# The second product of a ConvNeXt V2 block in 15 block products instead of 18, with the response normalisation applied to its input

## The chip, the cores and the metric

The kernel runs on one core of one Trainium2 chip. The metric is device time in microseconds (us) for one execution. All engines of the core work on their own instruction streams and wait for each other by semaphores: TensorE (matmuls), VectorE, ScalarE, GpSimd and SyncE, which here only issues transfers. In the profile they are PE (with PEld for the loads of stationary weights), DVE, ACT, POOL and SP; L12 is line 12 of the kernel.

## The reference, cut to what matters

Eight images of 384 channels and 32 x 32 positions pass through two layers in fp32. Layer 0 is a transformer block; layer 1 is a ConvNeXt V2 block. The change is mostly in the last lines of layer 1.

```python
# layer 0, per image, xf = positions x channels
x1 = attention(layernorm(xf)) + xf             # 8 heads of 48
h  = gelu(layernorm(x1) @ w_fc1.T + b_fc1)     # 384 -> 1536
x  = x1 + h @ w_fc2.T + b_fc2                  # 1536 -> 384
# layer 1, per image
y = depthwise_conv_7x7(x) + dw_b
y = layernorm(y)
y = gelu(y @ w1 + b1)                          # 384 -> 1536
gx = sqrt(sum(square(y), over the positions))  # one per channel
nx = gx / (mean(gx over channels) + 1e-6)
y = grn_gamma * (y * nx) + grn_beta + y        # response normalisation
out = x + y @ w2 + b2                          # 1536 -> 384
```

The response normalisation multiplies each of the 1536 channels by one factor, 1 + gamma * nx, known only when the whole image's gelu is done. grn_beta is folded into b2 once, in image 0.

## The kernel before, in words

Channels lie on the 128 partitions, positions along the free dimension: 384 channels are 3 tiles, 1536 are 12, an image has N = 1024 positions in two halves of NH = 512. A matmul is 128x128 weights by 128x512 activations. The loop `main` (L1442) takes the images in order; image b runs layer 0: `qk` (L442), `attention` (L537), `mlp` (L760) with fc1 and then `fc2` (L783), `keep` (L913, which stores x in DRAM). Then layer 1 of image b-1 runs: `grn_up` (L950, w1 and gelu), `values` (L472, the v projection of the next image) and `grn_down` (L1143, w2). The depthwise convolution of image b is 147 taps of 128x1024 on VectorE (L936), spread under the TensorE work of the next image. Images 6 and 7 go through w2 by `grn_down_straight` (L1023), 72 matmuls an image.

The order of the instructions is written out when the program is built. `Flow` (L111) keeps a clock that advances by U = 0.857 us for each 128x512 matmul emitted; chains of small steps (Python generators) yield how long they want to wait, and are continued when the clock has come that far. A paced chain counts its waits from when it was due, `flow.finish` emits all that is left of a chain at once. So what an engine does next is fixed by the planner's clock, not by who is ready.

Two fast block schemes save matmuls. `fc2` cuts h into three parts of four tiles by two halves of positions (b11 to b32) and computes 15 products of four matmuls each, p0 to p14, with sums of weight blocks (`FORMS`, L73) made once in image 0 by `prepare` (L1225) and kept in DRAM as s_fc2. The products' other operands are sums of activation blocks: e, f, g, h and d in the code, with e', f', f'', h' and g' here for the later values that overwrite them. VectorE makes those with pairs of 128x1024 sums (`both_pairs`, L816), or a GpSimd transfer adds one block to another in place (`adding`, L823). `grn_down` calls `down` (L671) instead: the third rows straight (24 matmuls) and seven products of six. Its operands t1 and t3 are differences by ScalarE (times -1) and a GpSimd accumulating transfer (`difference`, L661); t2 and t4 are VectorE's. The factors of the response normalisation are applied to w2: `scaled` (L1117) multiplies six weight tiles by them on VectorE as they come, and `grn_sums` (L1127) adds four sums of the scaled weights. `grn_scale` (L1095) makes the factors.

`down` adds x as residual from six loads of 256 KB (`load` in `grn_down`), adding the bias as it goes (L1153), and stores each block when it is complete. SyncE issues weight loads into a ring of nine tiles (`Weights`, L249), x and residual loads and stores in program order. PSUM results of products alternate between a pool of two double banks and a pool of four.

## Time and profile before

| what | value |
|---|---|
| median of 3 runs | 3422.79 us (3420.5 to 3424.79) |
| the profiled execution, its own time | 3430.41 us |
| its span | 3428.6 us |
| TensorE busy | 3362.1 us, 98% |
| VectorE busy | 2496.0 us, 73% |
| ScalarE busy | 1372.7 us, 40% |
| GpSimd busy | 142.2 us, 4% |
| transfers | 259.53 MB, mean 76 GB/s |

A group of instructions is given by line, engine and operation, then what it writes and reads, its count, its busy time and the mean length of one; the idle time before it and what released it follow. In the timeline a line is start, length, engine, line, operation, with the idle time just before it and its releaser in brackets. A matmul of 128x512 in fp32 shows as two records of TensorE (some records can be missing). The chain of waits follows the last instruction back to what released it; pieces in order of time are start, length, what. The busy table gives a stretch's bounds, its length, and the busy time and count of PE, PEld, DVE, ACT and POOL, then the granted TensorE clock, the share of the transfer engines and GB/s.

### The profile page before, as it was taken

The numbers are of one execution on the slowest core, as the hardware profiler recorded it, in microseconds if no ns is written. First come the engines' busy times: TensorE is split into PE (matmuls) and PEld (weight loads), VectorE is DVE, ScalarE is ACT, GpSimd is POOL, SyncE is SP. The second block draws the span as 40 slices with busy tenths as digits, with TensorE's granted clock in tenths as the row PEclk, the third lists the DMA queues.
The fourth block names the chain that finished last, engine by engine and source line by source line (L and its number), as shares of the span: only waits on it lengthen the run. The fifth ranks groups of instructions, "written<-read, shape, count | busy, mean of one in ns | idle before, by whom it ended". The sixth has DMA issues, their size and how long they took to land.

```text
span 3428.6 us, 36855 instructions
## 1 busy us (share of the span) xinstructions
PE 3362.1 (98%) x14194; PEld 1441.4 (42%) x14194; DVE 2496.0 (73%) x3040; ACT 1372.7 (40%) x1814; POOL 142.2 (4%) x155
## 2 busy tenths in 40 slices
PE   8999999999999999999999999999999999999999
PEld 3334434443344433444334443344434444344455
DVE  3343888777878778778787786977879679959950
ACT  2442353333534245341543515525154342531631
POOL 0201000000000000000001000010000000000000
PEclk9999999999999999999999999999999999999999
DMA  3415201641026410353005430054300642013231
GB/s 103 150 56 123 65 17 36 164 105 39 21 60 156 101 26 21 83 155 89 17 16 118 129 82 19 13 132 121 82 13 23 156 105 68 14 53 87 65 91 54
DMA packets 138952, 259.53 MB, mean 76 GB/s; under 512 B 33424, under 2 KB 35856, under 8 KB 138384
## 3 DMA queue, kind: packets, MB, share of 16 engines
q1 hardware_dynamic: 109424, 191.69, 18.8%
q0 software_dynamic: 28768, 62.92, 9.8%
q8 instruction: 114, 1.87, 0.2%
q10 hardware_dynamic: 576, 2.48, 0.2%
q14 instruction: 70, 0.57, 0.1%
HBM read 168.68 MB, written 30.41 MB: 58 GB/s over the span
## 4 chain that ended last, share of the span: by engine, by line
PE 81%; DVE 10%; DMA 2%; issue 1%; SPq 1%; ACT 1%; POOL 0%; DVEq 0%; POOLq 0%; ACTq 0%
PE fc L345 11%; PE s L548 10%; PE o L568 10%; PE h L352 10%; PE fc_p L352 9%; PE qk L332 5%; PE o L1043 4%; PE o_S L352 4%; PE o_straight L704 4%; PE v L477 3%; PE proj L491 3%; DVE acc L936 3%; DVE wqkv L936 3%; PE o_A L352 3%; PE h_last L1087 2%; PE ln_var L401 1%
## 5 line engine op out<-in xcount | busy, mean ns | idle before, releaser
L936 DVE SCALAR_TENSOR_TENSOR acc<-pad,vec,acc 128x1024 f32<-128x1024 f32 x1008 | 1230.9, 1275 | 0.0
L557 ACT ACTIVATE p<-s 128x1024 f32<-128x1024 f32 x512 | 523.2, 1023 | 390.4 <-PE s L548 390.0
L548 PE MATMUL s<-qk 48*64 48x512 f32 x4096 | 537.5, 593 | 1.7 <-ACT qk L451 1.5
L568 PE MATMUL o<-p,v 64*64 64x512 f32 x4096 | 531.7, 591 | 0.0
L345 PE MATMUL fc<-xn,fc 128*128 128x512 f32 x1152 | 503.3, 595 | 1.3 <-DVE x L758 1.2
L345 PEld LDWEIGHTS fc<-xn,fc 128*128 128x128 f32 x1152 | 218.5, 190 | 280.3 <-issue 272.8
L352 PE MATMUL fc_p<-hid,fc 128*128 128x512 f32 x728 | 323.4, 595 | 9.5 <-issue 9.5
L985 DVE TENSOR_TENSOR y<-h,y 128x512 f32<-128x512 f32 x288 | 198.4, 691 | 112.6 <-PE h L352 101.7
L548 PEld LDWEIGHTS s<-qk 48*64 48x64 f32 x4096 | 152.4, 133 | 295.9 <-issue 272.2
L568 PEld LDWEIGHTS o<-p,v 64*64 64x64 f32 x4096 | 157.1, 133 | 284.5 <-issue 279.6
L364 ACT ACTIVATE hid<-fc,bfc_f 128x512 f32<-128x512 f32 x192 | 130.8, 686 | 361.1 <-PE fc L345 360.9
L352 PEld LDWEIGHTS fc_p<-hid,fc 128*128 128x128 f32 x728 | 138.0, 190 | 186.4 <-issue 185.7
L332 PE MATMUL qk<-xn,wqkv 128*128 128x512 f32 x480 | 207.4, 592 | 0.0
L352 PE MATMUL h<-acc,w_A 128*128 128x512 f32 x432 | 204.0, 592 | 0.0
L936 DVE SCALAR_TENSOR_TENSOR wqkv<-pad,vec,wqkv 128x416 f32<-128x416 f32 (+1 forms) x288 | 193.4, 744 | 0.6
L451 ACT ACTIVATE qk<-qk,bqk 128x1024 f32<-128x1024 f32 x40 | 44.5, 1114 | 352.6 <-PE qk L332 352.6
L509 DVE TENSOR_TENSOR attn<-o,attn 128x512 f32<-128x512 f32 x64 | 44.1, 688 | 152.4 <-ACT attn L507 152.4
L491 PE MATMUL proj<-attn,wproj_sb 128*128 128x512 f32 x288 | 129.7, 603 | 11.2 <-DVE attn L535 11.2
L332 PEld LDWEIGHTS qk<-xn,wqkv 128*128 128x128 f32 x480 | 91.1, 190 | 114.1 <-issue 113.8
L477 PE MATMUL v<-wqkv,xn 128*128 128x384 f32 x384 | 129.0, 495 | 0.6 <-DVE xn L413 0.6
L352 PEld LDWEIGHTS h<-acc,w_A 128*128 128x128 f32 x432 | 82.1, 190 | 103.3 <-issue 99.0
L704 PE MATMUL o_straight<-y,w_A 128*128 128x512 f32 x288 | 124.6, 592 | 0.0
(254 smaller groups left out, 3299.2 us busy)
## 6 DMA issues: line engine op xcount, KB each, us to landing
w_A<-in_w SPq DMA_DIRECT2D x108, 384.0 KB, 3.2
fc<-s_fc SPq DMA_DIRECT2D x91, 256.0 KB, 2.8
hid<-hid POOLq DMA_DIRECT2D x42, 512.0 KB, 5.9
fc<-in_wfc SPq DMA_DIRECT2D x54, 384.0 KB, 3.4
xn<-in_x SPq DMA_DIRECT2D x16, 768.0 KB, 9.1
x<-in_x SPq DMA_DIRECT2D x16, 768.0 KB, 14.4
kept<-x SPq DMA_DIRECT2D x8, 1536.0 KB, 5.9
res<-kept SPq DMA_DIRECT2D x42, 256.0 KB, 3.5
```

The costliest lines, as they stand in the source:

```text
L332: nc.tensor.matmul(out=ps[:, half(h)], lhsT=lhsT(k), rhs=rhs(k)[:, half(h)], start=(k == 0), stop=(k == nk - 1),)
L345: nc.tensor.matmul(out=ps, lhsT=lhsT(k), rhs=rhs(k)[:, half(h)], start=(k == 0), stop=(k == nk - 1))
L352: nc.tensor.matmul(out=bank, lhsT=lhsT, rhs=rhs, start=k == 0, stop=k == len(pairs) - 1)
L477: nc.tensor.matmul(out=ps[:, :C], lhsT=xn[:, k, t * P : (t + 1) * P], rhs=wv_sb[:, k, :], start=(k == 0), stop=(k == CT - 1),)
L491: nc.tensor.matmul(out=ps, lhsT=wproj_sb[:, m, ct * P : (ct + 1) * P], rhs=attn[:, m, :], start=(m == 0), stop=(m == CT - 1),)
L548: nc.tensor.matmul(out=s[64 * i : 64 * i + 64, j, :], lhsT=kT[64 * j : 64 * j + HD, m, k0 : k0 + 64], rhs=qT[64 * j : 64 * j + HD, m, half ...
L557: nc.scalar.activation(p, s, AF.Exp)
L568: nc.tensor.matmul(out=outs[i][64 * j : 64 * j + 64, :], lhsT=v[keys, t, at : at + 64], rhs=p[keys, j, :], start=(t == 0), stop=(t == KT - 1),
L704: nc.tensor.matmul(out=straight[:, n, :], lhsT=a(key)[k], rhs=block(s, n)[k], start=s + k == 0, stop=s == 1 and k == h - 1,)
L936: nc.vector.scalar_tensor_tensor(dst, window, tap, dst, ALU.mult, ALU.add)
L985: nc.vector.tensor_tensor(dst, bank, part, ALU.add)
L1043: nc.tensor.matmul(out=ps, lhsT=tiles[k], rhs=y(k, part), start=(k == 0), stop=(k == HT - 1))
```

## The change

The change has five parts.

1. w2 of images 0 to 5 goes through fc2's scheme. `fc2` becomes `by_thirds`, called for both; `down`, `grn_sums`, `first_difference` and `spare_blocks` are gone. For w2 it makes e itself (`made` is False).
2. `prepare` makes the block sums of w2 too, after all else, by the same code, into s_w2. The waits in it grow from 10 to 16 and from 12 to 18.
3. The factors multiply y instead of w2: `grn_scale` emits twelve ScalarE multiplications of 128x1024 by a per-partition factor, between the copies of the v projection that runs then and on into the w2 stage.
4. The residual is one load of 1.5 MB into a tile with x's tag, before `grn_up`; products are added into it, and its six blocks are stored. The load of the next image's x stands behind `grn_down` now.
5. In `by_thirds`, so in fc2 too, h and e' are emitted earlier (h after f, during p2; e' right behind h) and f' directly after p6's first addition, not after p7.

The pace of the convolution is 1.6 instead of 1.55 in image 0, 1.46 instead of 1.42 in image 6.

```diff
@@ plan_w2
-        if not fast:
-            return [((f"w2_{tag}", a), chunk(w2, c)) for c, a in enumerate(RAW)]
-        return [
-            ((f"w2_{tag}", a), chunk(w2, RAW.index(a)) if a in RAW else None)
-            for a in ("A31", "A32", "A11", "A12", "A21", "S4", "S2", "S3", "A22")
-        ]
+        if fast:
+            return plan_thirds(f"w2_{tag}", w2, s_w2)
+        return [((f"w2_{tag}", a), chunk(w2, c)) for c, a in enumerate(RAW)]
@@ fc2
-    def fc2(b, xt, hid, e, weights, wname):
+    def by_thirds(xt, hid, e, made, weights, wname, column, done, name):
...
+        making_e = None if made else flow.spawn(both_pairs(e, b11, b12, ALU.subtract), paced=True)
         n16 = copy(spare[:, 0, :], product(b12))
         bias(2, c31, product(b21))
-        f = b21
+        flow.finish(making_e)
+        f, h = b21, b11
         making_f = flow.spawn(both_pairs(f, e, b21, ALU.subtract), paced=True)
+        making_h = flow.spawn(after(making_f, both_pairs(h, e, b31, ALU.subtract)), paced=True)
         p = product(e)
+        making_e = flow.spawn(after(making_h, both_pairs(e, h, b12)), paced=True)
         op(c31, p, c31)
         op(c21, c21, p, ALU.subtract)
         bias(2, c32, product(b22))
         flow.finish(making_f)
         g = b22
         adding(g, f)
-        h = b11
-        making_h = flow.spawn(both_pairs(h, e, b31, ALU.subtract), paced=True)
-        making_e = flow.spawn(after(making_h, both_pairs(e, h, b12)), paced=True)
         n17 = copy(spare[:, 1, :], product(f))
         flow.finish(making_h)
         n15 = copy(temporary("n15"), product(h))
         flow.finish(making_e)
         adding(h, b32)
         p = product(e)
         op(n15, p, n15)
+        flow.finish(flow.spawn(both_pairs(f, f, b12)))
         bias(0, c11, p)
...
         bias(1, c22, product(g))
         adding(g, b32)
-        making_f = flow.spawn(both_pairs(f, f, b12), paced=True)
         op(c11, product(b31), c11)
-        flow.finish(making_f)
         op(n17, product(f), n17, ALU.subtract)
         making_f = flow.spawn(after(None, both_pairs(f, f, g, ALU.subtract), 2.0), paced=True)
...
@@ grn_scale
-        for key in first:
-            scaled(b, weights.at(wb, key), key, key in spare)
+        if y is None:
+            for key in RAW[:2]:
+                scaled(b, weights.at(f"w2_{tag}", key), key, key == RAW[1])
+            return
+        yield 1.5
+        for m in range(HT):
+            nc.scalar.mul(y[:, m, :], y[:, m, :], scale[:, m : m + 1])
+            yield 1.1
@@ grn_down
+    def load_kept(b, kept):
+        t = one.tile([P, CT, N], F32, tag="x", name=f"kept_{b}")
+        nc.sync.dma_start(out=t, in_=kept.rearrange("(c p) n -> p c n", p=P))
+        return t
+
+    def grn_down(b, y, xt, weights, tag, index):
+        e = [three.tile([P, 2, NH], F32, tag="p", name=f"w2_e_{b}_{i}") for i in range(2)]
 
         def done(r, n):
-            if (r, n) == (2, 1):
-                flow.finish(sums)
-            nc.sync.dma_start(out=image_of(out, index)[r * P : (r + 1) * P, half(n)], in_=res.pop((r, n)))
-            if queue:
-                load(*queue.pop(0))
...
-        down(y, y1, weights, f"w2_{tag}", first, add, done, f"o2_{b}")
+            nc.sync.dma_start(out=image_of(out, index)[r * P : (r + 1) * P, half(n)], in_=xt[:, r, half(n)])
+
+        by_thirds(xt, y, e, False, weights, f"w2_{tag}", lambda r: b2[:, r : r + 1], done, f"o2_{b}")
@@ prepare
+        def forms(name, w, store):
...
+        yield from forms("fc2", wfc2, s_fc2)
         weights.release()
...
+        yield from forms("w2", w2, s_w2)
@@ main
+            if b == 0:
                 xt = load_x(b + 1, "x")
-            if b == 0:
                 flow.finish(preparing)
-                start_conv(b, 1.55)
+                start_conv(b, 1.6)
                 next_values(1)
                 continue
+            if b < B - 1:
+                xt = load_kept(b - 1, kept.pop(b - 1))
             flow.finish(state["norm3"])
             if b < B - 1:
-                y, y1, gx = grn_up(b - 1, acc, weights, b - 1)
-                start_conv(b, 1.42 if b == B - 2 else 1.8, 10)
-                scale = flow.spawn(grn_scale(b - 1, gx, weights, b - 1))
+                y, gx = grn_up(b - 1, acc, weights, b - 1)
+                start_conv(b, 1.46 if b == B - 2 else 1.8, 10)
+                scale = flow.spawn(grn_scale(b - 1, gx, weights, b - 1, y))
                 next_values(b + 1)
                 flow.finish(scale)
-                grn_down(b - 1, y, y1, kept.pop(b - 1), weights, b - 1, b - 1)
+                grn_down(b - 1, y, xt, weights, b - 1, b - 1)
+                xt = load_x(b + 1, "x")
```

## The prediction

> **What bounds the kernel.** The page's busy row and its chain first:

> ```profile
> PE 3362.1 (98%) x14194; PEld 1441.4 (42%) x14194; DVE 2496.0 (73%) x3040; ACT 1372.7 (40%) x1814; POOL 142.2 (4%) x155
> ...
> PE 81%; DVE 10%; DMA 2%; issue 1%; SPq 1%; ACT 1%; POOL 0%; DVEq 0%; POOLq 0%; ACTq 0%
> ```

> TensorE is busy 98%, and 9 tenths or more in every slice but the first: a matmul less is time less, a late operand is time more. Next the chain of waits through the second image's w2 (start, length, line, records):

> ```profile
> 1132.91 7.74 PE v L477 x24
> 1140.65 0.12 PE gxsum L1102 x2
> 1140.77 7.84 PE v L477 x24
> 1148.61 20.60 PE o_straight L704 x48
> 1169.21 10.30 PE o_A L352 x24
> 1179.51 20.60 PE o_S L352 x48
> 1200.11 5.15 PE o_A L352 x12
> ```

> Four pieces join without a gap into 56.65 us: 132 records, 66 matmuls of 128x512, two records each, so 0.858 us a matmul. The stage's rows in the busy table (us of PE, PEld, DVE, ACT, POOL), of the second and the sixth image:

> ```profile
> 1148.61:1205.26 56.65, 56.65 (x134) 25.08 (x133) 47.95 (x53) 4.24 (x5) 3.57 (x3) 1.00 0.43 109
> 2804.89:2861.54 56.65, 56.65 (x133) 25.08 (x133) 54.78 (x59) 4.24 (x5) 3.57 (x3) 1.00 0.43 109
> ```

> VectorE is nearly full here already, with the next convolution's taps, which can wait. Last, where TensorE does wait: fc2, in the timeline of one image:

> ```profile
> 1036.89 2.07 DVE L413 SCALAR_TENSOR_TENSOR acc<-acc,vec,ln_rstd 128x512 f32<-128x512 f32 x3
> ...
> 1038.88 2.07 DVE L413 SCALAR_TENSOR_TENSOR acc<-acc,vec,attn 128x512 f32<-128x512 f32 x3
> ...
> 1040.86 1.22 DVE L816 TENSOR_TENSOR fc_e<-hid 128x1024 f32<-128x1024 f32 x1
> ...
> 1042.14 1.98 PE L352 MATMUL fc_p<-fc_e,fc 128*128 128x512 f32 x4 [0.77 <-DVE fc_e L816]
> ...
> 1050.67 2.35 DVE L816 TENSOR_TENSOR hid<-hid 128x1024 f32<-128x1024 f32 x2
> ...
> 1051.99 4.53 PE L352 MATMUL fc_p<-hid,fc 128*128 128x512 f32 x10 [1.00 <-issue]
> ```

> The second half of e' sits behind six normalisation operations and costs 0.77; f' is made just before its product and costs 1.00 ("issue", but the product starts as f' is ready). Image 0 has 3.11 before the same product (at 332.19). The page's groups agree: 9.5 of idle before the L352 matmuls that read hid (6 x 1.00 + 3.1 and little else), 4.6 = 6 x 0.77 before those that read fc_e.

> [...] the trace has 1216 and 690. In a row they start 1.13–1.14 and 0.61 apart, read from the timeline.

> **Removed.** 18 products become 15 of four matmuls: 60 instead of 66, six images: 6 x 6 x 0.858 = −30.9. Scaling and summing weights on VectorE, the t1 and t3 differences and six residual loads go too; none holds TensorE in the rows above, so they only make room.

> **fc2.** In the shared code e' is queued straight after h, during the third product, ahead of the normalisations; f' follows p6's first operation rather than standing before p9. If both stalls go: 6 x (0.77 + 1.00) + 3.1 = −13.7.

> **Factors on ScalarE.** Let 0 be the start of the stage's first product (1148.61 above).

> ```profile
> 1141.74 0.17 DVE L1110 TENSOR_SCALAR gscale<-gscale 128x12 f32<-128x12 f32 x1
> ...
> 1142.85 0.48 ACT L485 COPY v<-v 128x384 f32<-128x384 f32 x1 [1.68 <-PE v L477]
> ...
> 1144.78 0.48 ACT L485 COPY v<-v 128x384 f32<-128x384 f32 x1 [1.46 <-PE v L477]
> ```

> The scale is ready at −6.7; ScalarE has 1.45 between v copies. No row has a 1024-wide multiply by a pointer; [...] the nearest rows have 1023 without and 1150 with a bias pointer. So one multiply fits after each of three copies, and of twelve the fourth ends at 1.75, the eighth at 5.9, the twelfth at 10.1. The first product (b12: tiles 0–3) reads the fourth at 3 x 0.858 = 2.6; the second (b21: 4–7) reads the eighth at 3.43 + 2.57 = 6.0. No spare, hence 0 to 0.2 a stage; I take 0. At a pitch of 1.2 it would be 0.9 a stage.

> **VectorE in the stage.** Fourteen 128x1024 sums are added. From the built order, after the bias of product 1 (its bank is full at 6.9, done about 7.1) up to the last half of f'', which the second half of product 12 reads, stand: 12 taps x 1.20 (1275 long, pitch from 31.18 for 26) = 14.4; 10 sums x 1.13 = 11.3; 5 scalar_tensor_tensor from PSUM x 0.67 = 3.35; 12 sums of 512 x 0.61 = 7.3; chained starts 0.4. Together 36.8, so 43.9. Product 12 starts at 41.2, its third matmul at 42.9: 1.0 late. In the sixth image the convolution is paced at 1.46, not 1.8, and 16 taps stand there: 4.8 more, 5.7 late. Sum: 5 x 1.0 + 5.7 = +10.7. The unknown is how tightly these run: 5% of 36.8 is 1.8 us an image either way, so 4 to 22. The taps behind it lose 6.5 to 9 us at the stage's end; 25 taps stand there before attention's first VectorE operation, which came with 15 us of VectorE idle before, so this stays covered (2.3 idle in image 7, where fewer sums stand).

> **GpSimd's accumulating transfers.** h += b32, g += f and g += b32, two halves each, replace the t1 and t3 ones. Issue takes 1.19; hid<-hid lands in 5.9 (page), y<-y in 5.0. [...] g += f is issued when product 3 is over (13.8), both halves land by 21–22; product 7 reads it at 24.0. h += b32 starts after product 5 (20.6), lands by 27, read at 34.3. g += b32 starts at 27.5, lands by 35, read by product 11 at 37.8. Spare 2 to 7: I take 0; a landing over 8.2, the longest seen, would cost what it exceeds.

> **Residual, loads, preparation.** The weights are 15 x 256 KB against 6 x 384 + 6 x 256 of weights and residual: equal bytes. The residual is one 1.5 MB transfer, ahead of grn_up, some 60 us before use. load_x moves behind the stage's stores on SP: a store (out<-res) takes 2.2 and x<-in_x lands in 14.4, so x is there some 25 us after the stage, and proj reads it a whole score and attention stretch later. The next qk's moves on SP stand behind its two issues; they are read by the scores, after qk's 60 matmuls (over 50 us), so 2 to 3 us of lateness is covered. Without that cover it would be those 2 to 3 an image. I take 0.

> **Preparation.** The sums of w2's blocks are made in image 0, where VectorE is nearly free under fc1 (5.91 of 52 us busy from 245 to 297):

> ```profile
> 245.00:297.00 52.00, 52.00 (x122) 22.91 (x121) 5.91 (x10) 21.16 (x29) 2.44 (x2) 1.00 0.21 46
> ```

> The order has all their VectorE work ahead of fc2's first bias, and two of GpSimd's fc2_e transfers queued behind stores and loads of w2 blocks: before, preparation ended about 245; its waits grow by 12 matmuls' time for fc2 and 42 for w2, to about 290–300, and fc2 starts at 296.3. It just fits: I take 0, and 5, once, as the end of the range.

> **Sum.** −30.9 − 13.7 + 10.7 = −33.9 against the profiled execution's 3430.4 (span 3428.6 and 1.8 around it): 3396.5. The median of the runs, 3422.8, is 7.6 lower: 3388.9.

> **Rivals.**
> (a) The fc2 stalls stay: something else is late there, the normalisations moved behind e' or the accumulations into f. Against it, those results are read only after fc2; for it, a stall is often handed on. −30.9 + 10.7 = −20.2: 3402.6.
> (b) VectorE bounds the w2 stage: demand in it is 16.0 (sums of 1024) + 4.0 + 12.8 + taps, and everything after product 9 needs its order kept; taps emitted ahead of sums make each 1.2 later. At 5 us in each image: −30.9 − 13.7 + 30 = −14.6: 3408.
> (c) No stall at all, the order being tighter than I sum: −44.6: 3378.
> (d) Slower. TensorE waits before f'' (or for g) by more than 44.6/6 = 7.4 us an image: the first five would have to be 6.4 later than I sum, five or six taps more ahead of f'', or a landing of 15 us for g += f. Nothing in the profile shows such a landing; the tap count is read from the order[...]. At 9 us an image: +9.4, 3432.
> (e) The change doesn't do what it says: it does, the order has 60 matmuls in the stage.

> **Chances.** Mine, 3381–3397: 0.53. (a) 0.15, (b) 0.17, (c) 0.09, slower (d) 0.06. 0.2% is 6.8 us, about what a measurement of this kernel can tell from no change; the far edge of (b), beyond 3416, holds 0.05, of which 0.04 is within it and 0.01 slower. So faster 0.89, same 0.04, slower 0.07. The range takes in (a), all but the tail of (c), and (b) up to its middle: 0.04 left out below, 0.15 above: 3377 to 3409.

> **What would show it.** The stage 51.5 us plus a wait of about 1 before product 12's third matmul, put down to VectorE's sum; 5 to 6 in the sixth image; none before product 1. In fc2 the rows with 0.77, 1.00 and 3.11 gone. Image 0's fc2 starting as before. What makes it wrong: a wait on g or h (transfers), on y (ScalarE), on the fc2's first product in image 0 (preparation), on moves of qk (load_x ahead of them on SP), or several us at each f''.

## The result and the profile after

The changed kernel takes 3375.72 us (median; 3372.85 to 3378.29) against 3423.79 us for the kernel before beside it: a ratio of 0.9861, 95% interval 0.9844 to 0.9878. That is 48.1 us faster by the medians, where 33.9 were forecast, and 1.3 us below the lower end of the range; of its four executions one (3378.29) lies above that end and three below. The profiled executions are 3374.66 and 3430.41 us, 55.8 us apart. The busy row and the chain's shares of the page after:

```profile
PE 3323.2 (99%) x14122; PEld 1424.9 (42%) x14122; DVE 2551.5 (76%) x3089; ACT 1422.2 (42%) x1868; POOL 155.7 (5%) x181
...
PE 83%; DVE 14%; DMA 1%; ACT 1%; issue 1%; SPq 0%; POOL 0%; DVEq 0%; ACTq 0%; POOLq 0%
```

TensorE is still the bound, now at 99%. VectorE has more to do although the scaling of the weights is gone, and holds 14% of the chain instead of 10%.

The w2 stage of the second image, in the timeline of TensorE, and the stage's rows in the busy table, second and sixth image:

```profile
1124.69 7.06 PE L351 MATMUL o_p<-y,w 128*128 128x512 f32 x16
1131.59 3.60 PE L351 MATMUL o_p<-w_e,w 128*128 128x512 f32 x8
1135.02 10.46 PE L351 MATMUL o_p<-y,w 128*128 128x512 f32 x24
1145.32 3.60 PE L351 MATMUL o_p<-w_e,w 128*128 128x512 f32 x8
1148.76 19.05 PE L351 MATMUL o_p<-y,w 128*128 128x512 f32 x44
1168.37 8.85 PE L351 MATMUL o_p<-y,w 128*128 128x512 f32 x20 [0.57 <-DVE y L727]
```

```profile
1124.69:1177.06 52.37, 51.80 (x122) 22.63 (x121) 49.09 (x53) 12.07 (x14) 7.11 (x6) 1.00 0.64 151
2754.69:2811.84 57.15, 53.72 (x122) 22.89 (x121) 55.08 (x58) 12.07 (x14) 7.11 (x6) 0.97 0.60 140
```

One wait, put down to VectorE's y. Twenty records, ten matmuls, follow it; fifty matmuls are done, so it is product 12's third. The stage is 52.37 us, 0.87 over 60 x 0.858 = 51.5; the sixth is 5.65 over, with a granted clock of 0.97. VectorE's operations around the wait, in its timeline:

```profile
1164.17 1.21 DVE L727 TENSOR_TENSOR y<-y 128x1024 f32<-128x1024 f32 x1
1165.31 0.68 DVE L727 TENSOR_TENSOR kept<-o_p,kept 128x512 f32<-128x512 f32 x1
...
1167.11 1.21 DVE L727 TENSOR_TENSOR y<-y 128x1024 f32<-128x1024 f32 x1
1168.24 1.27 DVE L847 SCALAR_TENSOR_TENSOR acc<-pad,vec,acc 128x1024 f32<-128x1024 f32 x1
```

The second half of f'' ends at 1168.3, 43.6 after the stage's start (43.9 was summed), and the matmul starts at 1168.37. In the sixth image both halves come late (timelines of TensorE and VectorE):

```profile
2799.03 3.63 PE L351 MATMUL o_p<-y,w 128*128 128x512 f32 x4 [2.94 <-DVE y L727]
2803.15 8.85 PE L351 MATMUL o_p<-y,w 128*128 128x512 f32 x20 [0.49 <-DVE y L727]
...
2801.88 1.21 DVE L727 TENSOR_TENSOR y<-y 128x1024 f32<-128x1024 f32 x1
```

The four records between the two waits took 3.63 us, at a granted clock of 0.50 (from 2799.22 to 2802.63), but this cost nothing of its own: the second half of f'' ends 48.4 us after the stage's start, where 42.9 was needed, and this is the stage's loss. ScalarE's multiplications, in its timeline, fit where they were put:

```profile
1119.46 1.15 ACT L1024 ACTIVATE y<-y,gscale 128x1024 f32<-128x1024 f32 x1
...
1125.27 9.46 ACT L1024 ACTIVATE y<-y,gscale 128x1024 f32<-128x1024 f32 x9
```

Each takes 1.15, nine take 9.46, so 1.04 apart. The profile before has no such multiplication, so it did not show the length and the pitch behind the forecast ends; here the fourth ends 1.73 after the stage's start, the eighth 5.88 and the twelfth 10.04, within 0.06 of 1.75, 5.9 and 10.1, and the same in all six stages within 0.01. No product waits for one.

fc2 and proj in the page's groups after (idle time last):

```profile
L351 PE MATMUL fc_p<-hid,fc 128*128 128x512 f32 x728 | 320.3, 592 | 0.0
...
L351 PE MATMUL o_p<-y,w 128*128 128x512 f32 x624 | 274.4, 596 | 6.3 <-DVE y L727 6.3
...
L490 PE MATMUL proj<-attn,wproj_sb 128*128 128x512 f32 x288 | 127.3, 595 | 0.8 <-DVE attn L534 0.8
```

fc2's 9.5 are gone, w2 has 6.3 in all, and proj's idle time is 0.8. Its row before, which the prediction did not read, has the largest idle time of all TensorE's groups there:

```profile
L491 PE MATMUL proj<-attn,wproj_sb 128*128 128x512 f32 x288 | 129.7, 603 | 11.2 <-DVE attn L535 11.2
```

With the starts of each stage on TensorE as marks, the 55.8 us of the two profiled executions fall into these stretches:

| stretch | before, us | after, us | difference | forecast |
|---|---|---|---|---|
| start to fc2 of image 0 | 296.29 | 287.30 | −9.0 | 0 |
| fc2 of image 0 | 60.47 | 57.51 | −3.0 | −3.1 |
| qk to fc2 of image 1 | 229.23 | 226.27 | −3.0 | 0 |
| fc2 of images 1 to 6 | 58.93 each, one 59.29 | 56.65 each | −14.0 | −10.6 |
| w2 of images 0 to 4 | 56.65 each | 52.37 each | −21.4 | −20.7 |
| w2 of image 5 | 56.65 | 57.15 | +0.5 | +0.6 |
| qk of image 7 to layer 1 after it | 298.94 | 292.69 | −6.3 | 0 |

Fc1 of image 6, 0.4 longer, makes up the rest. The stage that the change is about came out as forecast, 20.9 against 20.2 by these rows. The surprise lies elsewhere: 9.0, 3.0 and 6.3 us in places that were costed at nothing, and 3.3 us more in fc2.

### The profile page after: what moved, and what is told of

The parts are those of the page before. It is cut to its first block, busy times and chain, and to the rows that moved or that the text cites. A ratio compares the mean times of both kernels' runs of the same rounds, so it can differ in the third digit from the quotient of the medians.

```text
span 3372.8 us, 36885 instructions
## 1 busy us (share of the span) xinstructions
PE 3323.2 (99%) x14122; PEld 1424.9 (42%) x14122; DVE 2551.5 (76%) x3089; ACT 1422.2 (42%) x1868; POOL 155.7 (5%) x181
## 3 DMA queue, kind: packets, MB, share of 16 engines
q0 software_dynamic: 30848, 69.74, 10.6%
## 4 chain that ended last, share of the span: by engine, by line
PE 83%; DVE 14%; DMA 1%; ACT 1%; issue 1%; SPq 0%; POOL 0%; DVEq 0%; ACTq 0%; POOLq 0%
PE s L547 12%; PE o L567 12%; PE fc L344 12%; PE fc_p L351 10%; PE h L351 10%; PE qk L331 6%; DVE acc L847 5%; PE v L476 4%; PE o L950 4%; PE proj L490 3%; PE o_p L351 3%; DVE wqkv L847 3%; PE h_last L994 2%; DVE y L727 1%; PE ln_var L400 1%; PE qk_last L344 1%
## 5 line engine op out<-in xcount | busy, mean ns | idle before, releaser
L556 ACT ACTIVATE p<-s 128x1024 f32<-128x1024 f32 x512 | 523.5, 1024 | 390.4 <-PE s L547 390.0
L351 PE MATMUL o_p<-y,w 128*128 128x512 f32 x624 | 274.4, 596 | 6.3 <-DVE y L727 6.3
L351 PEld LDWEIGHTS o_p<-y,w 128*128 128x128 f32 x624 | 117.8, 190 | 158.7 <-issue 128.3
L450 ACT ACTIVATE qk<-qk,bqk 128x1024 f32<-128x1024 f32 x40 | 44.6, 1114 | 238.7 <-PE qk L331 238.7
```

The lines of the kernel that those rows point to most:

```text
L351: nc.tensor.matmul(out=bank, lhsT=lhsT, rhs=rhs, start=k == 0, stop=k == len(pairs) - 1)
L556: nc.scalar.activation(p, s, AF.Exp)
```

## The experiments

Each difference below is of medians against the kernel before in the same comparison (3423.4 to 3425.8), if nothing else is said. A difference from the changed kernel, or between two versions of it, is one of medians of mostly different comparisons and can be off by some 2 us for that; the stages of the profiles are the finer measure.

**The kernel before, profiled again.** No edit.

> The kernel before, unchanged, profiled once more. Theory: the waits of proj on attn in images 0, 1 and 7 (3.78, 1.53, 1.68, 4.21 us before) come from the order in which VectorE and the load queue get their instructions, so they return within 0.5 us each and the span is 3426 to 3430 us. Rival: they come from when small transfers happen to land in one execution; then they differ by 1 us or more, and the span is nearer 3420.

It took 3426.11 us, span 3424.3. Of the four waits, image 7's came back as 4.11; image 1's 1.68 was gone; image 0's were 2.47 and 3.15 instead of 3.78 and 1.53. So the first two images differ by some us from one execution to the next, and the rows of one trace there are not the change's. From image 1's fc2 to image 7's fc1 the two executions agree stage by stage within 0.02 us. So image 7's wait comes back with the program, as in the theory, and the others vary, as in the rival.

**fc2's order alone.** The old places of h, e' and f' further down go.

```diff
         making_f = flow.spawn(both_pairs(f, e, b21, ALU.subtract), paced=True)
+        making_h = flow.spawn(after(making_f, both_pairs(h, e, b31, ALU.subtract)), paced=True)
         p = product(e)
+        making_e = flow.spawn(after(making_h, both_pairs(e, h, b12)), paced=True)
...
         op(n15, p, n15)
+        flow.finish(flow.spawn(both_pairs(f, f, b12)))
```

> The kernel before with only fc2's new order (h, e' and f' emitted earlier). Theory: it removes all of fc2's waits, and each wait cost more than its idle time, since the matmuls after it restart slower: 2.28 us in each of images 1 to 6 (0.36 more in one) and 2.96 in image 0, so 17 us less than before (3407). Rival: only the idle time shown is won, 13.7 us (3410). Second rival: fc2's gain came from something else in the change (loads, preparation): 0 to 3 us.

3406.73 us, 16.9 less (ratio 0.9958, 0.9943 to 0.9972), as the theory had it; the stage rows give 17.0. fc2 is 56.65 in each of images 1 to 6 and 57.52 in image 0. No product waits any more; in image 0 a normalisation sum now waits 1.83 in between. A wait of 0.77 and one of 1.00 had cost 2.28, not 1.77, so about 0.26 more at each. Four records without a wait before them and the four after e', in the timeline of the kernel before:

```profile
1039.48 1.88 PE L352 MATMUL fc_p<-fc_e,fc 128*128 128x512 f32 x4
1042.14 1.98 PE L352 MATMUL fc_p<-fc_e,fc 128*128 128x512 f32 x4 [0.77 <-DVE fc_e L816]
```

In an unbroken row a record starts every 0.429 but is shown 0.59 long, so four show as 1.88 and the idle time before the next one is counted 0.16 late. Of the 0.26, this is 0.16; only the other 0.1 is a slower start.

**The paces alone.**

```diff
-                start_conv(b, 1.55)
+                start_conv(b, 1.6)
...
-                start_conv(b, 1.42 if b == B - 2 else 1.8, 10)
+                start_conv(b, 1.46 if b == B - 2 else 1.8, 10)
```

> The kernel before with only the two paces of the convolution changed (1.55 to 1.6 in image 0, 1.42 to 1.46 in image 6). Theory: the paces move taps past attention's and normalisation's operations on VectorE in images 1 and 7, and that is where 3.0 and 6.2 us went: 9 us less, the waits of proj in images 1 and 7 (1.68 and 4.21) gone or under 1. Rival: these waits vary from one execution to the next: 0 within 2 us.

3422.57 us (ratio 0.9998, 0.9989 to 1.0007), so the rival holds. Image 7's wait is 4.58. Image 1 did gain some: from qk to fc2 the seven profiles with the old pace have 227.4 to 229.4, 228.3 in the mean, the eleven with the new one 225.3 to 226.8, 226.2 in the mean.

**The preparation's waits alone.**

```diff
-        yield 10.0
+        yield 16.0
...
-        yield 12.0
+        yield 18.0
```

> The kernel before with only the two waits of the preparation longer (10 to 16, 12 to 18). Theory: it moves the bias folds of image 0 past attention's end, so fc2 of image 0 starts 6 to 9 us earlier: 6 to 9 us less. Rival: the 9 us come from w2's block sums standing in image 0, or from one execution: 0 within 2 us.

3422.30 us (ratio 0.9991, 0.9984 to 0.9998). proj's two waits in image 0 are gone and fc1 there takes 72.02 instead of 78.2 to 78.6, as in the changed kernel, but the bias folds before it (matmuls of one column) wait 3.05 and 3.40, where the two profiles of the kernel before have 1.86 and 2.22, or 2.50 alone. Some 1 to 3 us are left of the 9.0. All profiles together, but for the two of the experiments with fetches, put the way from the start to image 0's fc2 at 289.7 to 296.3 us in the six with the old waits, 293.7 in the mean, and at 286.8 to 292.4 in the ten with the longer ones, 289.7 in the mean. So about 4 of the 9.0 are the edit's, and the rest is how the two executions fell.

**All of these together, w2 as before.** The three edits above in one kernel.

> The kernel before with fc2's order, the two paces and the two waits of the preparation, that is, everything but w2's new scheme. Theory: the parts add, 16.9 + 1.0 + 2 to 3, so about 3403; proj's wait of 4.1 to 4.6 us in image 7 is still there, because it comes from w2's longer stage in the planner's order; the changed kernel's remaining 27 are w2's 20.9 and this wait. Rival: the wait in image 7 goes with the three together, and this is at 3397.

3402.94 us, 21.4 less (0.9935, 0.9918 to 0.9952), as the theory had it. fc2's order gives 16.9 of it, paces and preparation 4.5, a difference of two medians with intervals of several us. Image 7's wait of proj is still 4.21 (the reason given for it, w2's longer stage, falls with the experiment on fetches below). So w2's new scheme is worth 48.1 − 21.4 = 26.7 us, of which 20.9 are its six stages.

**The changed kernel with the old paces.** The edit of the paces, undone.

> The changed kernel with the old paces (1.55 and 1.42). Theory: image 7's wait of proj stays under 1 us, since the six matmuls less shift the order there; image 1 loses 1 to 2 us, the sixth w2 stage has its taps 3% closer and loses 0 to 1.2: 1 to 3 us more than the changed kernel, 3377 to 3379. Rival: the pace is what freed image 7; then 5 to 6 us more there, 3382.

3383.61 us, 7.9 more than the changed kernel, and neither theory: image 1's attention and fc1 lost 2.9, the sixth w2 stage 1.7 (58.81), image 7 3.9, though its wait of proj was gone. By the medians the paces are worth 1 us beside the old w2, not to be told from nothing, and 7 to 8 beside the new one.

**f'' ahead of product 10's sums.**

```diff
         p = product(h)
+        if not made:
+            flow.finish(making_f)
         op(c12, p, c12)
```

> The changed kernel with w2's f'' finished ahead of product 10's three sums. Theory: VectorE's queue ahead of f'' sets the wait at product 12; three sums of 0.6 and a tap of 1.2 less ahead of it remove the wait of 0.57 in images 0 to 4 (each stage 51.5 to 51.6, 0.8 less) and 3 us in the sixth: 7 us less than the changed kernel, 3369. Rival: f'' waits for g's transfer, not for VectorE's queue: no difference.

The five stages went to 51.53, as the theory said (their wait of 0.57 had cost 0.84: again some 0.26 more), but the sixth only to 56.44, image 7's attention came out 1.5 longer, and the median, 3376.10, is that of the changed kernel. In the profiled execution image 0 was 4.5 longer up to fc2, as it varies. TensorE runs through products 6 to 14 of the second image without a gap (timeline of that kernel):

```profile
1148.69 3.60 PE L351 MATMUL o_p<-w_e,w 128*128 128x512 f32 x8
1152.12 27.63 PE L351 MATMUL o_p<-y,w 128*128 128x512 f32 x64
```

**And fewer taps in the sixth stage.**

```diff
-            yield us * (1.35 if n <= CT * slow else 1.0)
+            yield us * (first if n <= CT * slow else 1.0)
...
-                start_conv(b, 1.46 if b == B - 2 else 1.8, 10)
+                start_conv(b, 1.4 if b == B - 2 else 1.8, 10, 1.8 if b == B - 2 else 1.35)
```

> As the last, and the convolution of image 6 slower in its first 30 taps (2.52 instead of 1.97 apart) and faster after (1.4), so that 12 taps instead of 16 stand ahead of the last f''. Theory: the sixth stage's wait goes too, 51.5 to 52, so 2.5 us less than the last one, if the convolution's taps, later by some 8 us, are still covered in image 7; 3366 to 3368. Rival: they are not, and image 7 gives back what the stage won.

3373.08 us. The sixth stage is 51.76: four taps fewer took its wait away, 4.7 us. In image 7 proj waits 3.80 again and fc1 is 4.7 longer, so the rival holds in time, though not by the convolution's end.

**One and three useless sums ahead of f''.**

```diff
+        if not made:
+            for i in range(1):
+                op(e[i % 2], h[i % 2], b12[i % 2])
         making_f = flow.spawn(after(None, both_pairs(f, f, g, ALU.subtract), 2.0), paced=True)
```

> The changed kernel with one useless VectorE sum of 128x1024 more ahead of w2's f''. Theory: VectorE's queue ahead of f'' is the limit, so the wait at product 12 grows by its whole 1.13 in each of six stages, 0.57 to 1.7: 6.8 us more, 3382.5. Rival (f'' is released by something else): 0 to 2 us more.

3382.75 us, 7.0 more; the first five stages are 53.50 instead of 52.37, just the 1.13 of a sum, and the sixth is 59.22, 2.1 more. VectorE's queue ahead of f'' is the limit.

> As the last with three such sums: 3.4 us in each of six stages, the waits in images 0 to 4 then 4.0 us. Theory: [...] 20 + 5 x 1.7 = 29 us more, 3404, and each of the first five stages 57.4. Rival: a wait costs its idle time alone: 20 us more, 3396, stages 55.8.

3400.21 us, 24.5 more, between the two. The theory's 1.7 in each of five stages is half the clock for one window of 3.41 us, the length measured below. Two of the first five stages are 55.8, as for idle time alone; the others are 56.5, 56.7 and 58.4. In the busy table, the second's and third's stretch at and behind the wait (granted clock third from the right):

```profile
1174.80:1177.80 3.00, 1.99 (x5) 0.68 (x5) 3.00 (x6) 0.00 (x0) 0.00 (x0) 1.00 0.10 39
1177.80:1182.00 4.20, 4.20 (x10) 2.00 (x11) 4.20 (x4) 0.00 (x0) 0.00 (x0) 1.00 0.69 190
1585.60:1588.60 3.00, 2.39 (x4) 0.68 (x4) 3.00 (x6) 0.00 (x0) 0.00 (x0) 0.75 0.10 38
1588.60:1593.00 4.40, 4.39 (x5) 1.85 (x6) 4.40 (x4) 0.00 (x0) 0.00 (x0) 0.50 0.48 123
```

Both waited 2.76 us. After one the clock stayed full, after the other it was halved. The length of a wait alone does not decide it in the other profiles either: 3.12 us before f' in image 0 (the kernel before with the paces) and 3.79 of proj in image 7 (with the preparation's waits) had the full clock behind them, and 1.67 in image 7's attention (the changed kernel with the old paces) had half.

The times of the clock's changes show more. In each of the eighteen traces of this case they lie whole multiples of 3.413 us apart, within 0.01, so time falls into windows of that length, and half the clock lasts one, two or three of them. In the kernel before, half the clock begins at 332.54 and at 3032.48 us, 791 windows apart. Here is one wait, that of 3.1 us before f' in image 0, in the kernel before and in the one with the paces alone (busy table, a row for each window):

```profile
329.12:332.54 3.42, 0.35 (x1) 0.30 (x2) 3.38 (x5) 0.00 (x0) 0.00 (x0) 1.00 1.09 250
332.54:335.95 3.41, 3.41 (x5) 1.35 (x4) 1.28 (x2) 0.00 (x0) 0.00 (x0) 0.50 0.57 145
```

```profile
320.61:324.02 3.41, 1.90 (x5) 0.57 (x3) 3.38 (x6) 0.53 (x1) 0.00 (x0) 1.00 1.05 208
324.02:327.44 3.42, 1.82 (x5) 0.89 (x6) 3.24 (x4) 0.00 (x0) 0.00 (x0) 1.00 1.10 242
327.44:330.85 3.41, 3.41 (x10) 1.50 (x8) 2.38 (x4) 1.65 (x3) 0.00 (x0) 1.00 0.11 33
```

Where the wait fell into one window, half the clock followed; where it was split over two, it didn't. fc2 of image 0 took 60.47 and 58.77: the 1.7 between them is half a window. Over all eighteen traces, from 108 us on to 20 us before the end, with matmuls of one column counted as idle and the others as busy for their pitch, all 61 windows of full clock in which TensorE was idle for 2.18 us or more had half the clock behind them, none with less than 1.92 had, and of the 32 between, eight had. Four of the five waits of 2.76 have their fullest window in this band, so for them it stays open.

**One tap in image 7.** The kernel before with this and the pace 1.6:

```diff
-                start_conv(b, 1.42 if b == B - 2 else 1.8, 10)
+                start_conv(b, 1.48 if b == B - 2 else 1.8, 10)
```

> The kernel before with the paces 1.6 and 1.48 (1.46 before this). In image 7 two taps then stand ahead of attention's last sum and two between it and its reciprocal, as in the changed kernel; with 1.42 and 1.46 it is three and none, or two and three. Theory: this one tap decides proj's wait: the reciprocal comes at 5.7 us after fc1's start instead of 8.1 to 8.3, the wait falls from 4.2 to 4.6 to under 1.2, and with the half clock after it image 7 is 5 us shorter; 3417 to 3418. Rival: something of w2's new scheme (transfers, residual, stage length) frees it; then 3422, the wait above 3.5.

3420.47 us (0.9983, 0.9976 to 0.9990), 5.4 less, about what the theory asked for, but not where it put it: proj still waits 3.35 and image 7's fc1 takes 144.51, while image 1 from qk to fc2 is at 225.33 instead of 227.5 to 229.2. The theory of the one tap falls.

**The version with that pace.** f'' early, the first 30 taps at 1.8 times:

```diff
-                start_conv(b, 1.4 if b == B - 2 else 1.8, 10, 1.8 if b == B - 2 else 1.35)
+                start_conv(b, 1.48 if b == B - 2 else 1.8, 10, 1.8 if b == B - 2 else 1.35)
```

> The version with f'' early and fewer taps in image 5's w2 stage, with the pace 1.48 instead of 1.4 after the first 30 taps of image 6, so that image 7 has two taps and two again around attention's last sum. Theory: w2's stages stay at 51.5 to 51.8 and image 7's wait goes: 4.5 to 5 us less than with 1.4, 3368. Rival: the slower pace is felt at the end of the convolution or in normalisation, and nothing is won: 3373 or more.

3371.05 us (ratio to the kernel before 0.9835, 0.9818 to 0.9852), the fastest here; all six stages are 51.53 and proj's wait is 0.73, but normalisation's matmuls now wait 1.42, 1.18 and 1.21 for VectorE, which has the later taps to do, and fc1 takes 144.17. The rival holds for the most part.

**TensorE later by six matmuls in image 5.** In the last version; in the kernel before the same ahead of its last product, A22:

```diff
+            if name == "o2_5" and n == 14:
+                for k in (0, 1, 2, 3, 0, 1):
+                    nc.tensor.matmul(out=bank, lhsT=w[:, k, :], rhs=pairs[k // 2][:, k % 2, :], start=True, stop=True)
             accumulate(bank, [(w[:, k, :], pairs[k // 2][:, k % 2, :]) for k in range(4)])
```

> The last version with six matmuls of image 5's last w2 product done twice (5.15 us of TensorE, the order of all other engines unchanged), so that TensorE reaches image 7 later by what the wait in the changed kernel's sixth stage cost. Theory: from this stage to image 7's second block VectorE's taps and attention's chain set the time, not TensorE, so a delay of TensorE here takes the place of the waits there: the stretch from the stage's start to layer 1 of the last images stays within 1.5 us of 349.8, and the time is 3371 to 3372.5. Rival: TensorE sets it: 354.9, and 3376.

> The kernel before with the same: six matmuls of image 5's last w2 product done twice. Theory: the wait of proj in image 7 (4.1 to 4.6 us and the half clock behind it) shrinks by what TensorE comes later, the stretch stays at 355.6 to 357, the time within 1.5 us of the kernel before. Rival: 5.15 us more, the stretch 360.7 and the wait as before.

3375.92 and 3430.42 us, 4.9 and 4.6 more; the stretches 354.15 and 361.22 instead of 349.77 and 355.59. Both rivals hold: TensorE's time counts in full there, and a wait in the sixth stage does not pay for one in image 7.

**Where the instructions are fetched.** In all sixteen profiles so far one step in image 7 follows one split. From the reciprocal of the pair of heads before the last to its product with r on VectorE (L515 to L534; L516 to L535 in the kernel before) small transfers of 4 to 96 KB follow each other. With the old w2 this took 6.2 to 6.6 us, with the new 5.5 to 5.8. With the old one, in all eight profiles, an instruction fetch of 0.02 MB (queue q8) falls between them, 1 to 4 us ahead of image 7's fc1; with the new one, in all eight, none of q8 does, and the nearest comes 10 to 12 us ahead. The kernel before has 114 such fetches for twice 14194 matmuls and weight loads, about 249 to a fetch, so they go with TensorE's instructions. In the attention of its image 7, five in a row start 13.54 to 13.75 us apart (2906.96 to 2961.56), and the busy table has 128 weight loads in each of these four stretches, so some 256 with their matmuls. Another queue's fetch of about 0.01 MB (q14) falls into the step with the new w2 and does not make it longer. The wait of proj hangs on this step and on the taps: with three taps ahead of attention's last sum it was 3.80 without a fetch of q8. Matmuls at the start move it:

```diff
         load_wqkv()
+        bank = o_tile("small")
+        for i in range(40):
+            nc.tensor.matmul(out=bank[:, :1], lhsT=ones, rhs=ones[:, 0:1], start=True, stop=True)
         ln_table()
```

> The kernel before with 40 matmuls of one column added at the start, while TensorE waits for the first image: 160 instructions of TensorE more ahead of everything. Theory: TensorE's instructions are fetched in pieces of 256 by transfers of 0.02 MB, every 14 us in attention, which is one pair of heads; in the old scheme a fetch falls 2 us before image 7's fc1, onto the small r transfers (landing 2.6 to 3.8 instead of 1.9 to 2.3), in the new one 11 us before it, since 36 matmuls less stand ahead. 160 instructions move it from -2 to about -11: r lands in 1.9 to 2.3, proj's wait in image 7 falls from 4.1 to 4.6 to at most 1.3, the stretch from fc1 to layer 1 from 144.2 to 139 to 140.5, and the time by about 5 us, to 3419. Rival: fetches have nothing to do with it; wait and stretch as before.

> The changed kernel with 24 such matmuls, 96 instructions. Theory: the fetch moves from 11 us before image 7's fc1 to 16 and 2 us before it, onto the r transfers: they land in 2.6 us or more, proj's wait grows from 0.77 to 3 to 4.5, the stretch from 139.2 to 143 to 144.5, the time to 3380. Rival: as the changed kernel, 3376.

proj in image 7, in TensorE's timeline: the kernel before, the same with 40 small matmuls, the changed kernel, the same with 24.

```profile
3032.60 7.89 PE L491 MATMUL proj<-attn,wproj_sb 128*128 128x512 f32 x14 [4.21 <-DVE attn L535]
```

```profile
3029.22 6.28 PE L491 MATMUL proj<-attn,wproj_sb 128*128 128x512 f32 x14 [1.21 <-DVE attn L535]
```

```profile
2978.42 6.28 PE L490 MATMUL proj<-attn,wproj_sb 128*128 128x512 f32 x14 [0.77 <-DVE attn L534]
```

```profile
2983.78 8.80 PE L490 MATMUL proj<-attn,wproj_sb 128*128 128x512 f32 x14 [4.22 <-DVE attn L534]
```

The fetch moved from 2 to 11 us ahead of fc1 and from 10 to under 1; the wait went from 4.2 to 1.2 and from 0.8 to 4.2, and the stretch from fc1 to layer 1 from 144.21 to 139.60 and from 139.16 to 145.14. The reciprocal-to-product step took 5.4 and 7.2. (The same step one pair of heads earlier has a fetch of q8 in it too wherever the wait is long in these four, and took 6.7 and 6.9 with it against 6.1 and 5.4 without, so part of the delay comes from there.) With each long wait goes the half clock: fourteen records took 7.89 and 8.80, and 6.28 after the short ones. The transfer view in 2 and 3 us around the last fetch, before and changed with 24:

```profile
q1 hardware_dynamic: 140, 0.17, 31.6%
q8 instruction: 1, 0.02, 4.4%
```

```profile
q1 hardware_dynamic: 193, 0.26, 32.9%
q8 instruction: 1, 0.02, 3.0%
```

So moving the fetches moved that wait, both ways and as forecast. A later start is not behind it: with 24 the first v starts only 0.6 us later. The times: 3423.60 with 40, as before, not the forecast 3419, since the first v starts 6.1 us later behind the small matmuls, which were to be hidden; 3385.24 with 24, 9.5 more than the changed kernel, 6.0 of it in image 7 and 1.7 in the sixth w2 stage, which took 58.84, with the half clock behind its second wait instead of the first. What joins a single fetch to transfers of 4 to 96 KB, whether it holds a queue or an engine of them, these runs don't show.

## Why the prediction was right and wrong

**The 60 matmuls, the factors, the transfers: right.** −30.9 holds. The factors cost nothing. The accumulating transfers landed later than read from the page before, 7.3 instead of 5.0 for y and 6.8 instead of 5.9 for hid at the median, and still no product waited for one. "Equal bytes" was wrong: the sum counts the residual on the old side alone. 90 weight loads of 256 KB take the place of 36 of 384, 1.5 MB more an image, and the residual's bytes stay. No product waited for these either, nor for the residual or the moved load_x.

**VectorE in the w2 stage: right in place and size.** 1.0 late in five images against 0.87, 5.7 in the sixth against 5.65, and one more sum ahead of f'' costs just itself. The 12 and 16 taps, ten sums of 1024 and twelve of 512 are in the timelines as counted; in a row the sums of 1024 take 1.21 us and start 1.13 to 1.14 apart, those of 512 take 0.68 and start 0.60 apart. Rival (b), 5 us in each image, and (d) fall; (c), no stall at all, falls too. That its 3378 is nearer to the measured 3375.72 than the forecast is chance: the stalls it left out were there, and the gain came from elsewhere.

**fc2: the stalls went, mis-sized by 3.2.** "−13.7" was the sum of idle times; the runs gave 16.9. The missing term is what a wait costs beyond the idle time shown, about 0.26, in part the way idle time is counted. That image 0 gave 3.0, close to the 3.1, is luck: with its wait went 1.7 of half clock (60.47 against the 58.77 of the same wait at full clock), and the new wait of 1.83 took about as much back. Rival (a) falls.

**Preparation, "I take 0, and 5, once, as the end of the range": this failed.** It was bounded on the side of a loss alone. The longer waits move the folds of image 0 on VectorE, and this, with the paces, which the prediction didn't cost at all, gave 4.5 by the medians (about 4 and 2 by the means of the profiles). A bound on the side of a gain too would have asked what else in image 0 stands where the waits move it.

**Image 7, "Last, where TensorE does wait: fc2": this failed too, by 5.5, the largest miss.** By the medians w2's scheme is worth 26.7, 20.9 of it in its stages, and image 7's stretches (298.15 with everything but w2, 292.69 after) hold 5.5. The list of TensorE's waits stopped at fc2. proj's row with 11.2 us of idle time stood on the page, larger than fc2's 9.5; 4.2 of it is image 7's, and no term of the sum has it. What freed it was where fetches fall, which no step about the edits would have given; that a wait of over 4 us hung on a chain of small transfers could have been read, and the lower end taken down by it.

Together: 3.2 + 4.5 + 5.5 + 0.7 in w2 = 13.9 of the 14.2 us between 33.9 and 48.1. Medians and single profiles are mixed in this sum, so that it closes within 0.3 is better than the terms are known.

## What to carry to other kernels

List every wait of the engine that bounds the kernel, also those that the edits don't touch, and price each by the time until the engine runs at its pitch again: here idle plus 0.26, and where one clock window of 3.41 us was idle for 2.18 us or more, half the clock on top, 1.7 us a window. Read stages whose length repeats to a hundredth as the measure of a change, and profile the kernel before twice to see which of its waits are its own. Where an engine is at its queue's limit, the order ahead of one operation decides: four taps were worth 4.7 us in a stage, and the taps' pace, worth 1 us before the change, was worth 7 to 8 after it.

## What was not expected of the hardware

Some 100 to 160 instructions of TensorE at the start of the program moved a fetch of 0.02 MB by about 10 us some 3000 us later, and with it a wait of 0.8 or 4.2 us came and went.
